# The 64-row remainder of the last product: two tiles of tokens in the two halves of TensorE's rows, in a kernel of attention, MLP and a block-quantised gated FFN

## The chip, the cores and the metric

The kernel runs on one core of a Trainium2 chip. The time is that of the device in microseconds (us) for one execution. The profiler gives the span from the first to the last instruction of one execution, in the same unit.

## What is computed

Eight sequences of 512 tokens with 256 features go through one layer, everything in float32. Per sequence: a layernorm; causal self-attention in which queries, keys and values are all the normed input; a residual layernorm; cross-attention to 64 context rows; another; an MLP of 256 to 1024 to 256 with relu; another; the sum with the input. Then comes the gated FFN, in which this case lies:

```
zq   = fp4(layernorm(x))                       # blocks of 16: scale, rounding to 8 levels, back
h    = silu(zq @ fp4(w_gate).T) * (zq @ fp4(w_up).T)      # 256 -> 704
out  = x + fp4(h) @ fp4(w_down).T                         # 704 -> 256
```

The inner width is 704 = 5 x 128 + 64. TensorE sums over its 128 rows, so the last product (704 to 256) is five full blocks of rows and a rest of 64.

## The kernel before, in words

**Tiling.** A sequence is a batch of four tiles of 128 tokens (NT = 4); there are B = 8 batches, hence 32 tiles. In the code I = 704, P = 128, D = 256, WI = I // P = 5 full blocks, RI = 64 the rest, NI = 6 blocks with the padded one.

**The last product (L1087 to L1112, `last`).** For each tile `product` issues NI = 6 matmuls into one bank of PSUM: the stationary operand is a block of hqT (704 inner features by 128 tokens, the turned and quantised h), the moving one a block of wd (inner features by 256 outputs). Block 6 holds 64 real rows and 64 rows of zeros in both. VectorE then adds the bank to x (L1102), and SyncE (SP) issues the store of the tile to the output (L1109). A float32 matmul stands in the profile as two MATMUL records, each after a LDWEIGHTS record of its own: 32 tiles x 6 x 2 = 384 records.

**How hqT is turned.** In batches 0 to 6 (`down`, L1038), ScalarE splits h into planes of 16 bits (L1047), SP stores the 704 columns of both planes to a DRAM buffer hd (L1053), and a transposing DMA reads hd back as hqT (L1058). There are three buffers hd; their last 64 columns are set to zero once at the start (`pads`, L1122, from a tile `nothing`, L384). In batch 7 TensorE turns h by products with an identity (L416 and L1078), and ScalarE evicts them (L1071, L1081, L1082); the zero rows of hqT come from three memsets at the start (L377). The weights w_down go the same way through hd into wd (L710, L715).

**What sets the order.** The kernel is written as operations with an engine, a cost and the buffers that they read and write. `Plan.order` (L190) simulates the engines with these costs and picks, on each engine, the operation with the lowest key whose inputs are there and whose buffers are free. The key comes from due times (`DUE`, L43, one for each batch and stage; stage 4 is the last product), drawn back through the chain of successors (`_keys`, L151), plus a push (L1139: the weights of the FFN; `LOAD_EARLY`, L42: the loads of x and context). Each kind of buffer has a number of homes, and some have quotas (L310 to L346). So costs, due times and numbers of homes fix the order in which the instructions of each engine stand; at run time each engine works through its list, waiting on semaphores. PSUM has eight banks of one kind, "bank", shared by all products.

The costs in the plan: `pe(cols)` (L56) is 0.429 us for a matmul of 256 moving columns; a tile's last product is 6 x 0.429 us. A turned block costs 0.112 us (L419).

One other product in this kernel doesn't fill TensorE's rows: `columns` (L721) turns the bias b1, an array of 8 rows by 128, once at the start (L730).

Of the kernel before, what the change touches and what calls it, by code (L numbers as in the profile page):

```python
# [12 lines left out]
U16 = mybir.dt.uint16  # L13
AF = mybir.ActivationFunctionType
ALU = mybir.AluOpType
# [4 lines left out]
P = 128  # L20
# [18 lines left out]
TURN = 2.6  # L39

BY_PRODUCTS = (4, 2, 1)
LOAD_EARLY = 2150.0  # L42
DUE = [  # L43
    [-1573.0, 346.0, 1086.0, -75.0, 155.0],
    [-342.0, 966.0, 145.0, -67.0, 387.0],
    [69.0, 825.0, -138.0, 835.0, 418.0],
    [2022.0, 515.0, -83.0, 958.0, 279.0],
    [963.0, 1398.0, 889.0, 514.0, -531.0],
    [101.0, -947.0, -373.0, -1174.0, -419.0],
    [-595.0, -1611.0, -583.0, -368.0, -313.0],  # L50
    [-1468.0, -811.0, -1127.0, -1471.0, -2197.0],
    [-2350.0],
]


def pe(cols):  # L56
    return 2 * max(0.109, cols * PE_PASS)
# [201 lines left out]
def kernel(  # L259
# [52 lines left out]
    z_homes = several("z", 8, [P, D + 2])  # L312
    plan.kind("y0", y0_homes)
    plan.kind("z", z_homes)
    plan.kind("zT", several("zT", 6, [P, ND, SZ]))
    plan.kind("turned", several("turned", 3, [P, ND, S]), ordered=False)
    plan.share("y0T", "turned", 3)
# [4 lines left out]
    plan.kind("xp", several("xp", 12, [P, NT, SZ]))  # L322
    xpT_homes = several("xpT", 1, [P, S])
    plan.kind("xpT", xpT_homes)
    plan.kind("hT", several("hT", 10, [P, S]))
    plan.kind("zq", several("zq", 1, [P, NT, D]))
    plan.kind("zm", several("zm", 2, [P, NT * D]), ordered=False)
    plan.kind("wide", several("h", 7, [P, NI * P]), ordered=False)
    plan.share("h", "wide", 5)
    plan.share("hm", "wide", 2)  # L330
    plan.share("wq", "wide", 5)
    hqT_homes = several("hqT", 3, [P, NI * P])
# [8 lines left out]
    plan.kind("ln", several("ln", 11, [P, 48]), ordered=False)  # L341
# [25 lines left out]
    ident = fixed("ident", [P, P])  # L367
# [5 lines left out]
        nc.gpsimd.memset(t[:SZ, D:], 1.0)  # L373
    for t in xpT_homes:
        nc.gpsimd.memset(t[SZ:, :], 0.0)

    for t in hqT_homes:  # L377
        nc.gpsimd.memset(t[RI:, WI * P :], 0.0)
    squares = fixed("squares", [P, D])
    mhalf = fixed("mhalf", [P, NT])  # L380
    nc.vector.memset(mhalf, -0.5)


    nothing = fixed("nothing", [P, 2, NI * P - I], U16)  # L384
    nc.gpsimd.memset(nothing, 0)


# [12 lines left out]
    wd = fixed("wd", [P, NI, D])  # L400

    plan.kind("const", ["const"] * 13, ordered=False)
    ready = {}
# [214 lines left out]
    def planes_of(v, n):  # L618
        return v.bitcast(U16).rearrange("p (g h k) -> p g h k", k=n, h=2)

    def weights():
# [4 lines left out]
        for j, w in enumerate((w_gate, w_up)):  # L626
            for half, groups in enumerate(((0, 1), (2, 3, 4))):
                v = plan.buf("wq")
                wide = len(groups) * D
# [17 lines left out]
                m = fp4(v, lambda v=v, n=n: v.ap[:, :n], "wq", n // BLOCK)  # L647
                g = len(groups)
                d = plan.buf("zd")

                def apart(v=v, m=m, n=n, wide=wide):
# [11 lines left out]
                    reads=[m], writes=[d], lag=1.1,  # L663
# [7 lines left out]
                    reads=[d], writes=[(ready["wgu"], (j, half))], lag=TURN,  # L671
                )
                if not half:
                    d = plan.buf("rest")
# [5 lines left out]
                        reads=[m], writes=[d], lag=1.5,  # L680
# [12 lines left out]
        for r in range(ND):  # L693
            v = plan.buf("wq")
            plan.op(
                "SP", 1.8, lambda v=v, r=r: nc.sync.dma_start(v.ap[:, :I], w_down[ts(r, P), :]),
                writes=[v],
            )
            m = fp4(v, lambda v=v: v.ap[:, :I], "wq", NBI)
            d = plan.buf("hd")  # L700
            plan.op(
                "ACT", act(2 * I),
                lambda v=v, m=m: nc.scalar.copy(
                    planes_of(m.ap[:, :I], I), halves(v.ap[:, :I], I)
                ),
                reads=[v], writes=[m],
            )
# [287 lines left out]
    def glu(b, xs, s):  # L995
# [5 lines left out]
        zT = plan.buf("zqT")  # L1001
# [36 lines left out]
        def down(t, h):  # L1038
            plan.stage = 4
            m = fp4(h, lambda h=h: h.ap[:, :I], "hm", NBI)  # L1040
            hqT = plan.buf("hqT")
            if b < B - 1:
                hd = plan.buf("hd")
                planes = lambda: m.ap[:, :I].bitcast(U16).rearrange("p (h k) -> p h k", h=2)
                plan.op(
                    "ACT", act(2 * I),
                    lambda: nc.scalar.copy(  # L1047
                        planes(), h.ap[:, :I].bitcast(U16).rearrange("p (k h) -> p h k", h=2)
                    ),
                    reads=[h], writes=[m],  # L1050
                )
# [12 lines left out]
            else:  # L1064
                turned_by_products(h, hqT)
            last(t, hqT)

        def turned_by_products(h, hqT):
# [16 lines left out]
            plan.op("ACT", 0.36, evict, reads=[pt], writes=[(hqT, 1)])  # L1085

        def last(t, hqT):  # L1087
            op = plan.buf("bank")

            def product(hqT=hqT, op=op):  # L1090
                for c in range(NI):
                    nc.tensor.matmul(  # L1092
                        op.ap[:, :D], hqT.ap[:, ts(c, P)], wd[:, c, :],
                        start=(c == 0), stop=(c == NI - 1),
                    )

            plan.op(
                "PE", NI * pe(D), product, reads=[(hqT, 0), (hqT, 1), ready["wd"]], writes=[op]
            )
            plan.op(  # L1100
                "DVE", 0.42,
                lambda t=t, op=op: nc.vector.tensor_tensor(  # L1102
                    xs.ap[:, t, :], op.ap[:, :D], xs.ap[:, t, :], ALU.add
                ),
                reads=[op], writes=[(xs, t)],
            )
            plan.op(
                "SP", 0.7,
                lambda t=t: nc.sync.dma_start(out[b, ts(t, P), :], xs.ap[:, t, :]),  # L1109
                reads=[(xs, t)],  # L1110
            )


        if b == B - 1:
# [7 lines left out]
    def pads():  # L1122

        for t in hd_homes:
            nc.sync.dma_start(t[:, :, I:], nothing)


    columns()
# [4 lines left out]
        writes=[ready["w1"]],  # L1133
# [47 lines left out]
```

## Time and profile before

| what | value |
|---|---|
| time, median of 3 runs | 584.24 us (583.91 to 584.69) |
| the profiled execution: its own time | 584.01 us |
| the profiled execution: its span | 582.0 us |
| TensorE busy | 570.7 us, 98% of the span |
| VectorE, ScalarE, GpSimd busy | 77%, 62%, 11% |
| the last product (L1092): records | 384 matmuls, 86.7 us busy |
| one of them: record / start to start | 380 ns / 215.8 ns |
| share of the 16 DMA engines | 45.6% |

PE in the profile is TensorE's matmuls, PEld its weight loads, DVE VectorE, ACT ScalarE, POOL GpSimd, SPq the queue of SyncE, which issues all the DMAs here. A form such as 128\*64 gives the rows and columns of TensorE's array that an instruction uses. Matmuls are pipelined: a record of 380 ns overlaps the next, so the price of one in a stream is the distance between two starts. The chain of waits gives it: twelve records of L1092 take 2.59 us there, 215.8 ns each. The profile calls "chain" the work that ended last, followed back from the last instruction; an engine that is in the chain for 96% of the span sets the time nearly alone.

### The profile page before, as it was taken

What the parts mean: (1) busy time and instruction counts of PE and PEld (TensorE: products, weight loads), DVE (VectorE), ACT (ScalarE), POOL (GpSimd) and SP (SyncE); (2) the same over time, 40 slices, a digit from 0 to 9 for tenths busy, and PEclk for the clock granted to TensorE, in tenths of its full rate; (3) what the DMA queues carried; (4) which work ended last, traced back from release to release, by engine and by line L of the source; (5) the groups of instructions that cost most, each with busy time, mean ns of one, the idle gap of its engine ahead of it and who ended that gap; (6) DMA issues with size and microseconds to landing.
All of it is one profiled execution on the core that took longest, in us unless ns stands there. A gap on an engine that the chain in (4) does not pass through costs nothing.

```text
span 582.0 us, 7151 instructions
## 1 busy us (share of the span) xinstructions
PE 570.7 (98%) x2273; PEld 409.2 (70%) x2273; DVE 447.5 (77%) x1125; ACT 359.6 (62%) x751; POOL 61.4 (11%) x102
## 2 busy tenths in 40 slices
PE   4999999999999999999999999999999999999997
PEld 2787485876697647678667777848578756877686
DVE  4799976979837998354998978978473897589892
ACT  4667948589748675444577777765953766345431
POOL 5222101022001000000201010000110100000000
PEclk9999999999999999999999999999999999999999
DMA  7930394462660257303338665655328042435421
GB/s 161 242 101 2 95 210 116 118 158 46 173 149 19 72 125 201 98 9 82 98 106 180 187 141 133 134 151 141 97 62 179 11 110 67 114 89 142 124 51 64
DMA packets 142581, 66.37 MB, mean 114 GB/s; under 512 B 107848, under 2 KB 142032, under 8 KB 142544
## 3 DMA queue, kind: packets, MB, share of 16 engines
q1 hardware_dynamic: 142544, 65.92, 45.6%
q8 instruction: 18, 0.29, 0.2%
q14 instruction: 19, 0.16, 0.1%
HBM read 9.90 MB, written 29.66 MB: 68 GB/s over the span
## 4 chain that ended last, share of the span: by engine, by line
PE 96%; DVE 1%; DMA 1%; ACT 1%; SPq 0%; POOL 0%; issue 0%; DVEq 0%
PE bank L1012 26%; PE bank L957 19%; PE bank L937 19%; PE bank L1092 14%; PE bank L797 6%; PE bank L764 5%; PE bank L915 2%; PE bank L876 2%; PE bank L416 2%; DMA z<-in_ctx_dram 1%; ACT squares L485 0%; SPq L356 0%; DVE x L554 0%; ACT turned L828 0%; DVE r L534 0%; POOL ln L500 0%
## 5 line engine op out<-in xcount | busy, mean ns | idle before, releaser
L1012 PE MATMUL bank<-wgu,turned 128*128 128x352 f32 x512 | 155.5, 459 | 0.0
L1012 PEld LDWEIGHTS bank<-wgu,turned 128*128 128x128 f32 x512 | 96.6, 190 | 50.4 <-issue 0.5
L957 PE MATMUL bank<-w,hT 128*128 128x256 f32 x512 | 112.6, 379 | 0.0
L937 PE MATMUL bank<-turned,w 128*128 128x512 f32 x256 | 111.5, 592 | 0.0
L957 PEld LDWEIGHTS bank<-w,hT 128*128 128x128 f32 x512 | 97.0, 190 | 14.5 <-issue 1.2
L937 PEld LDWEIGHTS bank<-turned,w 128*128 128x128 f32 x256 | 48.6, 190 | 57.4 <-issue 52.6
L1092 PE MATMUL bank<-wd,hqT 128*128 128x256 f32 x384 | 86.7, 380 | 0.0
L1092 PEld LDWEIGHTS bank<-wd,hqT 128*128 128x128 f32 x384 | 72.6, 190 | 12.5 <-issue 1.0
L600 DVE SCALAR_TENSOR_TENSOR h<-h,h 128x704 f32<-128x704 f32 (+2 forms) x76 | 66.7, 882 | 12.0 <-ACT h L594 11.7
L485 ACT ACTIVATE squares<-r,ln 128x256 f32<-128x256 f32 x96 | 48.8, 508 | 40.4 <-DVE ln L477 38.2
L500 POOL TENSOR_TENSOR ln<-ln,mhalf 128x4 f32<-128x4 f32 x32 | 36.5, 1139 | 351.7 <-DVE ln L493 351.7
L945 ACT ACTIVATE hT<-bank,cols 128x512 f32<-128x512 f32 x64 | 42.6, 682 | 17.0 <-PE bank L937 16.5
L1024 ACT ACTIVATE h<-bank 128x352 f32<-128x352 f32 x64 | 28.4, 457 | 34.8 <-PE bank L1012 34.4
L1047 ACT COPY h<-h 128x1408 uint16<-128x1408 uint16 x28 | 38.0, 1362 | 17.6 <-DVE h L607 17.5
L594 ACT ACTIVATE h<-h 128x704 f32<-128x704 f32 (+2 forms) x38 | 30.0, 789 | 26.6 <-DVE h L588 23.7
L968 DVE SCALAR_TENSOR_TENSOR r<-bank,r 128x256 f32<-128x256 f32 x32 | 13.4, 420 | 41.9 <-PE bank L957 41.9
L764 PE MATMUL bank<-turned 128*128 128x512 f32 (+3 forms) x128 | 38.1, 444 | 0.3 <-ACT turned L828 0.3
L797 PE MATMUL bank<-y,e 128*128 128x258 f32 x160 | 36.9, 382 | 0.1
L1031 DVE TENSOR_TENSOR h<-h,bank 128x352 f32<-128x352 f32 x64 | 32.1, 512 | 5.7 <-PE bank L1012 2.9
L607 DVE TENSOR_TENSOR h<-h,q 128x704 f32<-128x704 f32 (+2 forms) x38 | 33.5, 884 | 0.4
L588 DVE SCALAR_TENSOR_TENSOR h<-h,q 128x704 f32<-128x704 f32 (+2 forms) x38 | 33.5, 882 | 0.4
L797 PEld LDWEIGHTS bank<-y,e 128*128 128x128 f32 x160 | 29.9, 190 | 5.4 <-POOL e L784 0.5
(89 smaller groups left out, 664.5 us busy)
## 6 DMA issues: line engine op xcount, KB each, us to landing
zd<-zm SPq DMA_DIRECT2D x25, 512.0 KB, 2.9
hd<-h SPq DMA_DIRECT2D x30, 352.0 KB, 2.7
out_dram<-x SPq DMA_DIRECT2D x32, 128.0 KB, 1.7
x<-in_x_dram SPq DMA_DIRECT2D x7, 512.0 KB, 4.6
w<-in_L_xattn_w_dram SPq DMA_DIRECT2D x2, 1024.0 KB, 11.3
zd<-h SPq DMA_DIRECT2D x2, 384.0 KB, 2.8
h<-in_L_ffn_w_down_dram SPq DMA_DIRECT2D x2, 352.0 KB, 3.1
x<-in_x_dram SPq DMA_DIRECT2D x4, 128.0 KB, 2.2
```

The source lines that it names most:

```text
L485: lambda t=t: nc.scalar.activation(squares, view(t), AF.Square, bias=s.ap[:, 24 + t : 25 + t], accum_out=s.ap[:, 28 + t : 29 + t],),
L500: lambda: nc.gpsimd.tensor_tensor(s.ap[:, 36:40], s.ap[:, 32:36], mhalf, ALU.pow),
L588: lambda: nc.vector.scalar_tensor_tensor(blocks_of(view()), blocks_of(view()), TIE, each(rc()), ALU.mult, ALU.mult),
L600: lambda reverse=reverse, f=f: nc.vector.scalar_tensor_tensor(view(), mm(), LEAST, view(), ALU.max, f, reverse1=reverse),
L764: nc.tensor.matmul(sc.ap[:, :n], yT.ap[:, c, ts(k, P)], yT.ap[:, c, k * P :], start=(c == 0), stop=(c == ND - 1),)
L797: nc.tensor.matmul(av.ap[:, : D + 2], e.ap[:, ds(start[k] + (t - k) * P, P)], y0.ap[:, k, :], start=(k == 0), stop=(k == t),)
L937: nc.tensor.matmul(hp.ap, w1_sb[:, c, ts(f, P)], yT.ap[:, c, :], start=(c == 0), stop=(c == ND - 1),)
L945: lambda f=f, hp=hp, h=h: nc.scalar.activation(h.ap, hp.ap, AF.Relu, bias=b1_sb[:, f : f + 1]),
L957: nc.tensor.matmul(fp.ap[:, :D], hT[f].ap[:, ts(t, P)], w2_sb[:, f, :], start=(f == 0), stop=(f == NF - 1),)
L1012: nc.tensor.matmul(gp.ap[:, :HI], zT.ap[:, c, ts(t, P)], wgu[:, c, ds(j * I + n * HI, HI)], start=(c == 0), stop=(c == ND - 1),)
L1047: lambda: nc.scalar.copy(planes(), h.ap[:, :I].bitcast(U16).rearrange("p (k h) -> p h k", h=2)),
L1092: nc.tensor.matmul(op.ap[:, :D], hqT.ap[:, ts(c, P)], wd[:, c, :], start=(c == 0), stop=(c == NI - 1),)
```

## The change

1. **The product.** The five full blocks of a tile remain one operation of TensorE. The rest of 64 rows is no longer padded. When both tiles of a pair (0 and 1, 2 and 3) have their five blocks, a new operation `rests` issues for each a matmul over 64 rows only: the even tile's in rows 0 to 63 of the array, the odd tile's in rows 64 to 127, each into its own bank. The plan's cost of `rests` is 0.63 us. Only after it come the two additions on VectorE and the two stores of the output.
2. **Where the rest lies.** For odd tiles it must lie in rows 64 to 127 of hqT. The store into hd is then two DMAs instead of one (five blocks, and the rest 64 columns further on); for batch 7 the odd tile's second turned block takes 128 columns that end with the rest, and the eviction takes the upper half. In wd the rest lies in both halves: one more DMA for each of the two stores of w_down.
3. **The start.** The three memsets of hqT go; the zeros in hd are 128 columns wide instead of 64.
4. **The plan.** New due times, pushes, and numbers of homes: zT 6 to 7, xp 12 to 10, hT 10 to 9, wide 7 to 8, hm 2 to 3, wq 5 to 4, hqT 3 to 4, ln 11 to 13, y0T's quota 3 to 1.

```diff
-LOAD_EARLY = 2150.0
+LOAD_EARLY = 2634.0
 DUE = [
...
-    for t in hqT_homes:
-        nc.gpsimd.memset(t[RI:, WI * P :], 0.0)
...
-    nothing = fixed("nothing", [P, 2, NI * P - I], U16)
+    nothing = fixed("nothing", [P, 2, P], U16)
...
-                lambda m=m, d=d: nc.sync.dma_start(d.ap[:, :, :I], planes_of(m.ap[:, :I], I)[:, 0]),
+                lambda m=m, d=d: [
+                    nc.sync.dma_start(d.ap[:, :, :I], planes_of(m.ap[:, :I], I)[:, 0]),
+                    nc.sync.dma_start(
+                        d.ap[:, :, I:], planes_of(m.ap[:, :I], I)[:, 0, :, WI * P :]
+                    ),
+                ],
...
+                def store():
+                    if t % 2:
+                        nc.sync.dma_start(hd.ap[:, :, : WI * P], planes()[:, :, : WI * P])
+                        nc.sync.dma_start(hd.ap[:, :, I:], planes()[:, :, WI * P :])
+                    else:
+                        nc.sync.dma_start(hd.ap[:, :, :I], planes())
+
                 plan.op(
-                    "SP", 1.4, lambda: nc.sync.dma_start(hd.ap[:, :, :I], planes()),
+                    "SP", 1.4 + 0.5 * (t % 2), store,
...
             def rest(h=h, pt=pt):
-                for c in range(4, NI):
-                    cw = min(P, I - c * P)
-                    nc.tensor.transpose(pt.ap[:cw, ts(c - 4, P)], h.ap[:, ds(c * P, cw)], ident)
+                nc.tensor.transpose(pt.ap[:, :P], h.ap[:, ts(4, P)], ident)
+                lo = I - RI * (1 + t % 2)
+                nc.tensor.transpose(pt.ap[: I - lo, ts(1, P)], h.ap[:, lo:I], ident)
...
-                nc.scalar.copy(hqT.ap[:RI, ds(WI * P, P)], pt.ap[:RI, ts(WI - 4, P)])
+                half = ts(t % 2, RI)
+                nc.scalar.copy(hqT.ap[half, ds(WI * P, P)], pt.ap[half, ts(1, P)])
...
             def product(hqT=hqT, op=op):
-                for c in range(NI):
+                for c in range(WI):
                     nc.tensor.matmul(
                         op.ap[:, :D], hqT.ap[:, ts(c, P)], wd[:, c, :],
-                        start=(c == 0), stop=(c == NI - 1),
+                        start=(c == 0), stop=False,
                     )
...
+            pair.append((t, hqT, op))
+            if len(pair) < 2:
+                return
+            two = list(pair)
+            pair.clear()
+            def rests():
+                for t, hqT, op in two:
+                    half = ts(t % 2, RI)
+                    nc.tensor.matmul(
+                        op.ap[:, :D], hqT.ap[half, ds(WI * P, P)], wd[half, WI, :],
+                        start=False, stop=True,
+                    )
+            plan.op(
+                "PE", 0.63, rests, reads=[(q, 1) for _, q, _ in two],
+                writes=[o for _, _, o in two],
+            )
+            for t, hqT, op in two:
...
-            nc.sync.dma_start(t[:, :, I:], nothing)
+            nc.sync.dma_start(t[:, :, WI * P :], nothing)
...
-    plan.push = 5681.0
+    plan.push = 8884.0
```

More of the change, by code (lines that the diff above doesn't have):

```diff
@@ L41 @@
 BY_PRODUCTS = (4, 2, 1)
-LOAD_EARLY = 2150.0
+LOAD_EARLY = 2634.0
 DUE = [
[L44 to L52, printed above, removed]
+    [-1972.0, 451.0, 1026.0, -71.0, 390.0],
+    [-366.0, 1145.0, 287.0, -63.0, 448.0],
+    [-84.0, 957.0, -115.0, 759.0, 489.0],
+    [2198.0, 240.0, -81.0, 1231.0, 322.0],
+    [2074.0, 1527.0, 1434.0, 1260.0, -3.0],
+    [531.0, -18.0, 233.0, -763.0, 298.0],
+    [132.0, -1150.0, -257.0, 407.0, 387.0],
+    [261.0, 24.0, -783.0, -585.0, -670.0],
+    [-2984.0],
 ]
@@ L314 @@
     plan.kind("z", z_homes)
-    plan.kind("zT", several("zT", 6, [P, ND, SZ]))
+    plan.kind("zT", several("zT", 7, [P, ND, SZ]))
     plan.kind("turned", several("turned", 3, [P, ND, S]), ordered=False)
-    plan.share("y0T", "turned", 3)
+    plan.share("y0T", "turned", 1)
     plan.share("yT", "turned", 3, ordered=False)
@@ L321 @@
     plan.kind("r", several("r", 3, [P, NT, D]))
-    plan.kind("xp", several("xp", 12, [P, NT, SZ]))
+    plan.kind("xp", several("xp", 10, [P, NT, SZ]))
     xpT_homes = several("xpT", 1, [P, S])
     plan.kind("xpT", xpT_homes)
-    plan.kind("hT", several("hT", 10, [P, S]))
+    plan.kind("hT", several("hT", 9, [P, S]))
     plan.kind("zq", several("zq", 1, [P, NT, D]))
     plan.kind("zm", several("zm", 2, [P, NT * D]), ordered=False)
-    plan.kind("wide", several("h", 7, [P, NI * P]), ordered=False)
+    plan.kind("wide", several("h", 8, [P, NI * P]), ordered=False)
     plan.share("h", "wide", 5)
-    plan.share("hm", "wide", 2)
-    plan.share("wq", "wide", 5)
-    hqT_homes = several("hqT", 3, [P, NI * P])
+    plan.share("hm", "wide", 3)
+    plan.share("wq", "wide", 4)
+    hqT_homes = several("hqT", 4, [P, NI * P])
     plan.kind("hqT", hqT_homes)
@@ L340 @@
     plan.kind("zd", zd_homes, ordered=False)
-    plan.kind("ln", several("ln", 11, [P, 48]), ordered=False)
+    plan.kind("ln", several("ln", 13, [P, 48]), ordered=False)
     plan.kind("q", several("q", 6, [P, 3, 64]), ordered=False)
@@ L1064, in down, with turned_by_products @@
             else:
-                turned_by_products(h, hqT)
+                turned_by_products(t, h, hqT)
             last(t, hqT)
-        def turned_by_products(h, hqT):
+        def turned_by_products(t, h, hqT):
             transposed(
@@ L1075, in rest @@
             def rest(h=h, pt=pt):
-                for c in range(4, NI):
-                    cw = min(P, I - c * P)
-                    nc.tensor.transpose(pt.ap[:cw, ts(c - 4, P)], h.ap[:, ds(c * P, cw)], ident)
+                nc.tensor.transpose(pt.ap[:, :P], h.ap[:, ts(4, P)], ident)
+                lo = I - RI * (1 + t % 2)
+                nc.tensor.transpose(pt.ap[: I - lo, ts(1, P)], h.ap[:, lo:I], ident)
             def evict(pt=pt, hqT=hqT):
                 nc.scalar.copy(hqT.ap[:, 4 * P : WI * P], pt.ap[:, : (WI - 4) * P])
-                nc.scalar.copy(hqT.ap[:RI, ds(WI * P, P)], pt.ap[:RI, ts(WI - 4, P)])
+                half = ts(t % 2, RI)
+                nc.scalar.copy(hqT.ap[half, ds(WI * P, P)], pt.ap[half, ts(1, P)])
             plan.op("PE", 0.27, rest, reads=[h], writes=[pt], takes=[hqT])
             plan.op("ACT", 0.36, evict, reads=[pt], writes=[(hqT, 1)])
+        pair = []
         def last(t, hqT):
@@ L1090, in product @@
             def product(hqT=hqT, op=op):
-                for c in range(NI):
+                for c in range(WI):
                     nc.tensor.matmul(
                         op.ap[:, :D], hqT.ap[:, ts(c, P)], wd[:, c, :],
-                        start=(c == 0), stop=(c == NI - 1),
+                        start=(c == 0), stop=False,
                     )
             plan.op(
-                "PE", NI * pe(D), product, reads=[(hqT, 0), (hqT, 1), ready["wd"]], writes=[op]
-            )
-            plan.op(
[L1101 to L1105, printed above, removed]
-            )
[L1107 to L1111, printed above, removed]
+                "PE", WI * pe(D), product, reads=[(hqT, 0), (hqT, 1), ready["wd"]],
+                writes=[op],
+            )
+            pair.append((t, hqT, op))
[10 more added lines that the diff above has]
+                    )
+            plan.op(
+                "PE", 0.63, rests, reads=[(q, 1) for _, q, _ in two],
+                writes=[o for _, _, o in two],
+            )
+            for t, hqT, op in two:
+                plan.op(
+                    "DVE", 0.42,
+                    lambda t=t, op=op: nc.vector.tensor_tensor(
+                        xs.ap[:, t, :], op.ap[:, :D], xs.ap[:, t, :], ALU.add
+                    ),
+                    reads=[op], writes=[(xs, t)],
+                )
+                plan.op(
+                    "SP", 0.7,
+                    lambda t=t: nc.sync.dma_start(out[b, ts(t, P), :], xs.ap[:, t, :]),
+                    reads=[(xs, t)],
+                )
         if b == B - 1:
```

## The prediction

> **What bounds the kernel now.** I read the engines' shares first, then the chain that ended last, then who made TensorE wait, then the only place where TensorE works on fewer than 128 rows.
>
> ```profile
> PE 570.7 (98%) x2273; PEld 409.2 (70%) x2273; DVE 447.5 (77%) x1125; ACT 359.6 (62%) x751; POOL 61.4 (11%) x102
> ...
> PEclk9999999999999999999999999999999999999999
> ...
> PE 96%; DVE 1%; DMA 1%; ACT 1%; SPq 0%; POOL 0%; issue 0%; DVEq 0%
> ...
> L1092 PE MATMUL bank<-wd,hqT 128*128 128x256 f32 x384 | 86.7, 380 | 0.0
> ```
>
> TensorE is busy 98% of the span, makes up 96% of the chain, and runs at its full clock in all slices. The last product, L1092, never waits: 0.0 us idle before 384 records.
>
> ```profile
> PE bank L416 <- DMA z<-in_ctx_dram: 7.7, 2, 6.2
> ...
> PE bank L764 <- ACT turned L828: 0.3, 1, 0.3
> ```
>
> These two lines of the view of waits are all that TensorE waits for: 7.7 us for the context at the start, and 0.3 us once. In the chain TensorE runs from 10.8 to 578.8 us without a break, so the time moves one for one with the work on TensorE, and what the other engines do counts only where it makes TensorE wait, or at the two ends.
>
> **The work on TensorE.** In the chain twelve records of L1092 take 2.59 us, 215.8 ns from start to start. The padded sixth matmul is two of them, and a pair of tiles has four: 4 x 215.8 = 863 ns. There are 32 tiles, 16 pairs. The change takes these 13.8 us away and puts 16 operations `rests` in their place, each four records again of the same 256 columns, but over 64 rows. The whole question is how long one takes, and that has two unknowns.
>
> *Do the two halves run side by side?* No two neighbouring matmuls of this trace use different halves of the rows, so bound it: two slots of 215.8 ns if each record of one tile lies beside one of the other (432 ns), four if none does (863 ns). The order of issue decides between them. Each matmul is two records one behind the other, so the list is A first, A second, B first, B second. Matmul starts follow the program's order in this trace. Then A second must wait for A first, which holds the same rows; B first can start beside A second; B second must wait for B first. That is three slots, 647 ns, also the middle of the bounds. I take it.
>
> *What does the change of rows cost?* One instruction of this trace works on fewer than 128 rows, the turning of the bias (L730, 8 rows). These are lines of the timeline around it:
>
> ```profile
> 15.82 0.50 PE L764 MATMUL bank<-turned 128*128 128x128 f32 x3
> 15.93 0.19 PEld L764 LDWEIGHTS bank<-turned 128*128 128x128 f32 x1
> ...
> 16.24 0.14 PEld L730 LDWEIGHTS bank<-ident,c_rows 8*128 8x128 f32 x1
> 16.25 0.23 PE L730 MATMUL bank<-ident,c_rows 8*128 8x8 f32 x1
> 16.41 0.19 PEld L797 LDWEIGHTS bank<-y,e 128*128 128x128 f32 x1
> 16.41 0.70 PE L797 MATMUL bank<-y,e 128*128 128x258 f32 x2
> ```
>
> Columns: start, time, engine, line. Elsewhere the weights of the next matmul load as the present one starts: the load at 15.93 belongs to the last matmul of L764, which starts at 16.04 (end 16.32 less its 275 ns). The load for L730 doesn't start then, but 204 ns later, and L730's matmul with it; nor does the load for L797 run ahead, it starts at 16.41 with its own matmul. The next matmul of L797 starts only at 16.73 (end 17.11 less 0.38), 321 ns on where 217 is usual. From the start at 16.04 to that at 16.73 are 691 ns. Without L730 they would be 109 (usual for this form) + 217 = 326. So the excursion costs 365 ns, of which its own stream of 8 columns is 8/256 of 215.8, 7 ns. The other **358 ns** are two switches: the array runs empty (97 ns more than usual going in, about 53 coming out) and the weights load in the open (321 - 217 = 104 ns, twice). Neither load waited for data: the bias had landed at 10.4 us, and the part of `e` that L797's first matmul reads was done at 14.7.
>
> It is one place, and 8 rows, not 64; so bound it from both sides. The lower end is nothing: the 36 turned blocks of form 128\*64 (L416 and L1078) alternate with 128\*128 at the usual 109 ns, loads ahead, so a change of columns costs nothing. The upper end is 358 ns for each `rests`. I take 358, since L730 is the only row in which the number of *rows* changes, and it does so both ways.
>
> So a `rests` is 647 + 358 = 1005 ns where 863 stood: 142 ns more, x 16 = **+2.3 us**.
>
> Two rules of the Trainium skill bear on this. "TensorEngine Tiling (Array Packing)", section Tiling Modes, says that a change of the tiling mode drains TensorE, while a mere change of tile doesn't; it speaks against this change. L730 agrees (358 ns), the 128\*64 blocks don't. "TensorE: Matmul & The Clock Gate", Part 3, has matmuls on different rows start some 4 ns apart, with a span of about one matmul for the pack; no run here shows it. Taken for the whole pair, and without the drain, that would be 432 + 4 ns and -6.8 us. The sum above needs neither.
>
> **The other parts.**
> - *Order.* All due times and the numbers of homes change, so every engine's list does. From 10.8 us on the old order leaves TensorE 0.3 us idle, so a new one can gain no more than that there. It could lose: the even tile's bank is held until the odd tile's product is done (the chain has products of neighbouring tiles 9.5 to 16 us apart), so seven of eight banks turn over. A bank of L937 is filled in 859 ns and emptied by ScalarE in 682 ns (L945), so three suffice. I take 0, ends -0.3 and +1.0.
> - *The split store.* 14 odd tiles get one more DMA on SP, of the kind that takes 566 ns to issue (L1053, median), 7.9 us in all; behind it in SP's list stand the transposing read of the same tile, the other tiles' and outputs' DMAs. What hides it: hqT lands 4.0 us after its issue, and TensorE waits for none of the 28. The tightest, issued at 554.3, lands about 558.3, for a product at 560.6: 2.3 us of slack against 0.6. If all that cover were gone, 14 x 0.57 = 7.9 us would be the price; I take 0. The two further stores for w_down, pads of twice the width and the copies of batch 7 (same number, same widths) go with it, at 0.
> - *The waits of `rests`.* It needs both products, which stand ahead of it on TensorE and have already waited for both hqT. So nothing new can hold up what is queued behind it.
> - *The start.* Three memsets go from GpSimd, 0.5 us just ahead of its first power (L455 at 6.54), on which the first normed tiles hang (ScalarE, 7.50); the wider zeros give back some 0.2. TensorE waits for the fourth normed tile at 9.2 for 0.32 us. I take -0.2. With the new order of loads it may be -1.1 (TensorE's first y at 8.05, where the first tile is normed, instead of 8.77, and those 0.3) to +1.0 (two more DMAs ahead of the context, 0.4 to 0.6 us each).
> - *The end.* Before, the last addition (0.42 us) starts at 578.85 and the span ends at 582.0. Now tiles 2 and 3 finish together and VectorE adds them one behind the other. The first bank is ready one or two slots before the second, so the last addition moves by 0 to 0.42 us. I take +0.2.
>
> Sum against the profiled execution's 584.01 us: 2.3 + 0 - 0.2 + 0.2 = +2.3, **586.3 us**. The median before, 584.24, is 0.2 us above that execution, so the same number stands for the median. About 0.2% (1.2 us) is what a measurement of this kernel can tell from no change.
>
> **The rivals.**
> - *A. Switches cost as at L730, three slots*: the forecast, 585.4 to 587.4. **0.47.** (If the array empties in 53 ns both ways, 1.6 us instead of 2.3.)
> - *B. The switch to 64 rows is free, three slots*: 647 - 863 = -216 ns x 16 = -3.5 us, **580.5**. It is the case on the other side, and one mechanism: whether the first load over 64 rows, and the first over 128 after it, run ahead. It decides from 216 ns: a round trip cheaper than that makes the change a gain. For it: the free change of columns, and the plan's cost of 0.63 us for `rests`, near 647, where `pe(256)` = 0.429 is near the measured 0.432. Against it: L730. **0.28.**
> - *C. Switches cost, and the halves don't run side by side*: 863 + 358 - 863 = +358 x 16 = +5.7, 589.7. For it: no two matmuls of this trace run in one slot. **0.09.**
> - *D. Switches cost, and the halves overlap fully*: 432 + 358 = 790, -73 x 16 = -1.2, 582.8. Against it: the order of issue. **0.07.**
> - *E. The change doesn't do what it says*: no overlap, no price of switches: 584.0. **0.05.**
> - *F. Full overlap, free switches*: -6.9, 577.1. **0.04.**
>
> **The numbers.** Forecast A: 586.3. The range leaves out C, F and the ends of the rest: from B with 0.6 us of the start's lower end, 579.9, to A with the upper ends of the banks (+1.0) and the start (+1.2 over what I took), 588.5. Cases of both signs hold most of it: A alone is 585.4 to 587.4. Slower by over 0.2%: A but its lower edge, and C, 0.54. Within 0.2%: E, half of D, the edge of A, 0.10. Faster: B, F, half of D, 0.36.
>
> **What would show it.** In the timeline of the changed kernel, around a group of records over 64 rows: whether its first load starts with the last 128-row matmul (B) or some 0.3 us later (A); whether the third record starts a few ns after the second (three slots) or 216 ns (C); the distance from the first 64-row start to the next 128-row one. L1092's follower should have 320 records, and the 64-row line 64. TensorE must still have no wait in the middle of the span. The prediction is wrong if the loads run ahead, if the order of the four records isn't as I take it, or if TensorE starts to wait for banks.

## The result, and the profile after

| | before | after |
|---|---|---|
| time, median of 4 runs each on one chip | 584.47 us (583.91 to 584.74) | 588.25 us (587.62 to 588.27) |
| ratio, 95% interval | | 1.0063 (1.0046 to 1.0081) |
| the profiled execution: its time / its span | 584.01 / 582.0 us | 588.26 / 586.5 us |

The change makes the kernel slower by 3.8 us, more than a measurement can mistake. The forecast was 586.3, slower, with a range to 588.5, so direction and range held. The way to it didn't: two of its steps were wrong by 3 and 5 us, in opposite directions.

These are lines of the page after, those that answer to the ones shown of before. The last product is now L1105 (five blocks) and L1124 (the pair, `rests`).

```profile
PE 571.1 (97%) x2273; PEld 400.8 (68%) x2273; DVE 447.3 (76%) x1125; ACT 363.0 (62%) x753; POOL 61.3 (10%) x99
...
PEclk9999999999999999999999999999999999999999
...
PE 86%; DVE 4%; DMA 4%; ACT 3%; POOL 1%; SPq 1%; issue 1%; DVEq 0%; POOLq 0%; ACTq 0%
...
L1105 PE MATMUL bank<-wd,hqT 128*128 128x256 f32 x320 | 73.8, 381 | 0.0
```

TensorE's busy time is 0.4 us more, the span 4.5 us. TensorE makes up 86% of the chain where it made up 96%: DMA, VectorE and ScalarE have come into it. So the first place to look is not the new operation but who makes TensorE wait (columns: us in total, times, longest):

```profile
PE bank L412 <- DMA z<-in_ctx_dram: 7.2, 2, 5.1
PE bank L798 <- POOL e L785: 1.4, 1, 1.4
PE bank L1013 <- DMA turned<-zd: 1.3, 1, 1.3
PE bank L765 <- DMA turned<-zd: 0.8, 1, 0.8
PE bank L916 <- ACT xpT L901: 0.4, 1, 0.4
PE bank L938 <- DVE h L596: 0.4, 1, 0.4
PE bank L877 <- DMA turned<-zd: 0.2, 1, 0.2
```

The first line is the start, as before. Below it before had one wait of 0.3 us; now there are six, at 26.3 (POOL), 49.0 (xpT), 127.7, 340.1, 374.2 and 449.4 us, together 4.5 us. None is at `rests`.

Now the new operation itself, in the timeline around one pair (start, time, engine, line, records), first the matmuls, then the weight loads:

```profile
270.38 0.81 PE L1105 MATMUL bank<-wd,hqT 128*128 128x256 f32 x3
271.13 0.70 PE L1124 MATMUL bank<-wd,hqT 64*128 64x256 f32 x4
271.76 0.86 PE L1013 MATMUL bank<-wgu,turned 128*128 128x352 f32 x2
```

```profile
270.60 0.19 PEld L1105 LDWEIGHTS bank<-wd,hqT 128*128 128x128 f32 x1
271.12 0.30 PEld L1124 LDWEIGHTS bank<-wd,hqT 64*128 64x128 f32 x4 [0.33 <-issue]
271.76 0.59 PEld L1013 LDWEIGHTS bank<-wgu,turned 128*128 128x128 f32 x3 [0.33 <-issue]
```

The loads show the two switches, as the prediction's last part described them: the loads over 64 rows don't run ahead, they start with their own matmuls at 271.12, 0.33 us after the load before has ended; the next load over 128 rows waits 0.33 us again, until 271.76. Within the group the four matmul records start at 271.126, 271.132, 271.446 and 271.452 us: two together, and 314 ns later two together. That is two slots, not three.

To price the pair, I measure from the last start over 128 rows ahead of it to the first regular step behind it. The last L1105 starts at 270.816, and the second L1013 at 272.156 (271.76 + 0.86, less its 461 ns): 1340 ns, of which 216 for that L1105 and 296 for the first L1013 are usual. **828 ns** are the pair's. It splits so: 310 ns from the last L1105 to the first L1124, 94 more than usual, in which the array runs empty; 320 from the first to the third record, one slot of 216 and 104 of a weight load in the open; 310 from the third to the load of L1013, one slot and 94 of running empty again; and 400 from the first L1013 to the second, 104 more than usual, another open load. 94 + 320 + 310 + 104 = 828. Thirteen of the 15 pairs in the stream cost 828 to 831 ns; two, which are followed by turned blocks, 755. The padded form costs 863. The end of the last pair, where no switch back follows, is left out.

**Where the 4.5 us of span come from**, all against the profile before. The start is 0.34 us earlier (the first matmul of 512 columns at 10.44 us instead of 10.78). From there to the end of TensorE's last record are 4.4 us more; in them the pairs give back 0.9 us (13 x 33 ns, twice 108 ns, and 0.23 us for the last pair, behind which no switch back follows), so waits and gaps take 5.3 us more (the view of waits books 4.2 of it as waits). The end is 0.5 us longer (3.64 us from the end of TensorE's last record to the end of the span, 3.16 before). The sum, -0.3 - 0.9 + 5.3 + 0.5, is the span's growth to 0.1 us.

### The profile page after: what moved, and what is told of

The parts are those of the page before. It is cut to its first block, busy times and chain, and to the rows that moved or that the text cites. A ratio compares the mean times of both kernels' runs of the same rounds, so it can differ in the third digit from the quotient of the medians.

```text
span 586.5 us, 7179 instructions
## 1 busy us (share of the span) xinstructions
PE 571.1 (97%) x2273; PEld 400.8 (68%) x2273; DVE 447.3 (76%) x1125; ACT 363.0 (62%) x753; POOL 61.3 (10%) x99
## 4 chain that ended last, share of the span: by engine, by line
PE 86%; DVE 4%; DMA 4%; ACT 3%; POOL 1%; SPq 1%; issue 1%; DVEq 0%; POOLq 0%; ACTq 0%
PE bank L1013 23%; PE bank L958 19%; PE bank L938 19%; PE bank L1105 11%; PE bank L798 5%; PE bank L765 3%; DMA turned<-zd 2%; PE bank L916 2%; ACT squares L481 2%; PE bank L1124 2%; DMA v_beta<-in_L_xattn_beta_dram 1%; PE bank L877 1%; PE bank L412 1%; DVE r L909 1%; SPq L741 0%
## 5 line engine op out<-in xcount | busy, mean ns | idle before, releaser
L1013 PE MATMUL bank<-wgu,turned 128*128 128x352 f32 x512 | 156.7, 461 | 1.3 <-DMA turned<-zd 1.3
L1013 PEld LDWEIGHTS bank<-wgu,turned 128*128 128x128 f32 x512 | 96.1, 190 | 54.9 <-issue 3.4
L1105 PE MATMUL bank<-wd,hqT 128*128 128x256 f32 x320 | 73.8, 381 | 0.0
L1105 PEld LDWEIGHTS bank<-wd,hqT 128*128 128x128 f32 x320 | 60.1, 190 | 12.5 <-issue 2.5
L1025 ACT ACTIVATE h<-bank 128x352 f32<-128x352 f32 x64 | 28.4, 456 | 26.6 <-PE bank L1013 26.3
L765 PE MATMUL bank<-turned 128*128 128x512 f32 (+3 forms) x128 | 38.3, 447 | 0.8 <-DMA turned<-zd 0.8
```

The costliest lines, as they stand in the source:

```text
L765: nc.tensor.matmul(sc.ap[:, :n], yT.ap[:, c, ts(k, P)], yT.ap[:, c, k * P :], start=(c == 0), stop=(c == ND - 1),)
L1013: nc.tensor.matmul(gp.ap[:, :HI], zT.ap[:, c, ts(t, P)], wgu[:, c, ds(j * I + n * HI, HI)], start=(c == 0), stop=(c == ND - 1),)
L1105: nc.tensor.matmul(op.ap[:, :D], hqT.ap[:, ts(c, P)], wd[:, c, :], start=(c == 0), stop=False,)
```

## The experiments

My theory after the result: (1) a pair costs 830 ns because the halves overlap and two switches cost some 395; (2) the slowdown is the new order of the work, which makes TensorE wait, and not the pair. The rivals: the pairs' switches cause the waits; or three slots plus a cheaper switch make up 830; or the new stores on SP make the late transfers. All ratios are against the kernel before in runs on the same chip; the runs stand on several chips, so a difference between the medians of two of them is rougher than their ratios.

### What a pair costs: e1, e2

e1 keeps every list of the kernel after and takes `rests` over all 128 rows; e2 keeps 64 rows, but both tiles in the lower half.

```diff
-                        op.ap[:, :D], hqT.ap[half, ds(WI * P, P)], wd[half, WI, :],
+                        op.ap[:, :D], hqT.ap[:, ds(WI * P, P)], wd[:, WI, :],      # e1
-                    half = ts(t % 2, RI)
+                    half = ts(0, RI)                                               # e2
```

> The changed kernel with every engine's list of instructions as it is, but the operation `rests` multiplies over all 128 rows (its sums take in 64 stale rows, so its output is not the reference's). My theory now: the two halves run fully side by side, and a pair costs about 830 ns with its two switches of rows, against 863 ns over full rows; the rest of the slowdown comes from the order, where TensorE waits in the middle of the span for 5 to 6 us. So here: the switches are gone, a pair takes 863 ns, the waits stay: 588.5 to 589.2 us, 0.3 to 0.9 over the changed kernel. Rival, the three slots of the prediction (1005 ns a pair): 142 x 16 = 2.3 us less, 586.0. Rival, the waits come from the switches: they go, about 584.

> The changed kernel with the same lists, but both matmuls of `rests` use rows 0 to 63 (the odd tile's sum takes stale rows, so the output is not the reference's). If the halves really run side by side in the changed kernel, here they can't: four slots, 863 + about 395 of switches = 1260 ns a pair, 430 more, 6.9 us over 16, of which the waits in the middle can take up some: 591 to 595 us. If four records take two slots for another reason than the halves, a pair stays at 830 ns and the time at 588.3.

e1: 588.87 us, 1.008 (1.0065 to 1.0095). e2: 593.05 us, 1.0149 (1.0134 to 1.0164). The chain of waits through the same pair, first of e1, then of e2, then of the kernel after (start, us, line, records):

```profile
269.32 2.16 PE bank L1105 x10
271.48 0.86 PE bank L1123 x4
272.35 2.37 PE bank L1013 x8
```

```profile
269.09 2.16 PE bank L1105 x10
271.25 1.06 PE bank L1124 x4
272.31 2.56 PE bank L1013 x8
```

```profile
269.04 2.16 PE bank L1105 x10
271.19 0.63 PE bank L1124 x4
271.83 2.56 PE bank L1013 x8
```

The full rows take 0.86 us, and their loads run ahead: no switch. With both tiles in one half the starts are 320, 216 and 216 ns apart, four slots, and the entry grows by 0.43 us, exactly two slots. So it is the second half of the rows that saves two slots, not one; "three slots" is refuted, and so is a cheaper switch. The medians of e1 and of the kernel after are 0.6 us apart, but the intervals of their ratios overlap, so the worth of the pairs rests on the traces: 0.9 us for all 16, of which the end (3.20 us in e1, 3.64 in the kernel after) takes back 0.4.

The chain also shows a trap. Its entry of 0.63 us runs from the first record over 64 rows to the next load; the 93 ns of running empty stand with L1105, the open load with L1013 (2.56 us for eight records, where e1 has 2.37). The plan's 0.63 equals this number, and it is 0.2 us short of the price.

In e1 the waits are still there (POOL 1.6, turned 1.4, 0.7 and 0.5, xpT 0.4 us), all but the one of 0.4 us for `h`: they don't come from the switches. In e2, where TensorE needs 6.9 us more for its pairs, the time grows by only 4.8 us, and the waits at 340, 374 and 449 us shrink to 0.3 us or less; the one at 127.7, ahead of all pairs, stays (1.1 us). What TensorE waits for runs beside it at its own pace.

### How far the overlap goes: e7, e8

Each pair's two products are issued twice, in turn (A, B, A, B; e7) or grouped (A, A, B, B; e8).

```diff
-                for t, hqT, op in two:
+                for n, k in enumerate((0, 1, 0, 1)):      # e8: (0, 0, 1, 1)
+                    t, hqT, op = two[k]
```

> The changed kernel with the same lists, but `rests` issues its two matmuls twice, in the order A, B, A, B (the rest is counted twice in the output). If the two halves work through their own matmuls side by side: four slots, 864 + about 395 for the switches = 1260 ns, so a second pair within one change of rows costs 432 ns instead of 830. The time: 16 x 0.43 = 6.9 us more, less what the waits take up.

> As the run before, in the order A, A, B, B. The question is how far a matmul of one half passes those of the other that stand ahead of it. If it passes any: four slots, 1260 ns. If only the one record right ahead of it: six slots or nearly, 1475 to 1690 ns.

One execution each, so without an interval: 592.63 and 593.30 us. In the traces two pairs in one switch cost 1262 ns (e7) and 1268 (e8): one switch, four slots, both times. In e7 the starts are 6, 315, 6, 209, 7, 209 and 7 ns apart. In e8 the first record of B starts about 13 ns after the first of A, ahead of three records of A that stand before it in the program. (The records don't name their half; that two within 13 ns are one of each follows from e2, where records of one half stand 216 ns apart.) That is the point at which the forecast's order of issue failed: a matmul isn't held up by earlier ones on the other half. And the price of a switch is per excursion: a second pair in the same one costs 432 ns.

### Which part of the order: e3, e4, e9

The waits for `turned` (the turned zq) looked like a buffer that came free too late: the chain goes from TensorE's L765, which reads `turned`, to the DMA.

```profile
119.01 4.36 PE bank L798 x20
123.37 1.70 PE bank L765 x4
125.06 4.22 DMA turned<-zd
129.28 0.14 issue
129.42 1.42 PE bank L1013 x4
```

So e3 gives `turned` a fourth piece of memory, over which the three homes rotate. e4 takes the additional store of the odd tiles away (a rival: more DMAs on SP).

```diff
+                if k["of"] == "turned":                     # e3
+                    self.spare.append(b.home)
+                    b.home = self.spare.pop(0)
...
-                    if t % 2:                               # e4
+                    if False:
```

> The changed kernel with the same lists, but the buffers `turned` go round over four pieces of memory instead of three (the plan still counts three). Theory: three of the waits in the middle (at 127.7, 340 and 449 us, 2.8 us together) are transposing DMAs that start only when TensorE has read the last of the three buffers, and then take 4.2 to 4.5 us; with a fourth they start earlier: 585.5 us (584.8 to 586.5), the other waits stay. Rival, the queue of SP or the transfers themselves are late: 588.3, the waits stay.

> The changed kernel, but odd tiles store h in one DMA, as even ones do (their rest lands in rows 0 to 63, the product takes stale rows, so the output is not the reference's). Theory: the 14 extra DMAs cost TensorE nothing: within 0.5 us of 588.3. Rival, the split stores hold up SP's queue and so the transposing DMAs: 1 to 4 us less.

e3: 587.61 us, 1.0065 (1.0042 to 1.0089), the same waits (1.4, 0.9 and 0.3 us). My theory of the buffer fell. SP's own timeline in the kernel after shows what the chain's inferred releaser hides:

```profile
121.31 0.57 SPq L847 DMA_DIRECT2D zd<-zm  x1
125.06 1.78 SPq L852 DMA_TRANSPOSE turned<-zd  x1
```

The transposing read at 125.06 waits for the store of the same data, issued at 121.31. From there to the landing at 129.28 are 8.0 us, where the plan counts 1.9 + 1.1 + 1.8 + 2.6 = 7.4.

That store is itself late. Ahead of it in SP's list stands the transposing read of w_down (L716), and this waits 1.9 us for the second of the two stores (L708) that the change put in place of one. Two lines of the timeline, and L708 in the view of DMAs (KB, us to landing):

```profile
114.93 0.61 SPq L708 DMA_DIRECT2D hd<-h  x1
119.75 1.50 SPq L716 DMA_TRANSPOSE wd<-hd  x1
```

```profile
hd<-h SPq DMA_DIRECT2D x1, 32.0 KB, 4.3
```

The median of the 16 stores of this size is 2.3 us. In e7, whose lists are the same up to there, L708 lands after 2.4 us, L716 starts at 117.42, and the wait at 127.7 is gone. The DMA packets of the traces tell these runs apart: in the kernel after, e1, e2, e3, e4 and e8, all with that wait, a packet of 16 KB of the instruction queue starts between 116.8 and 117.3 us, and the last 16 packets of L708 start behind it (at 118.2 in the kernel after); in e7 and e9 it comes at 113.8 and 114.2, ahead of L708. That the one delays the other is not shown by a run of its own.

e4: 593.25 us, 1.0147 (1.0124 to 1.017). TensorE's waits at 26, 127.7, 340 and 449 us are all there (1.5, 1.1, 1.2 and 2.5 us), so the second stores of the odd tiles aren't their cause; the second stores of w_down stay in e4, and it says nothing of them. The time is longer for another reason. These are windows of the trace (us; busy time of PE, PEld, DVE, ACT and POOL; then the granted clock, the share of the DMA engines and GB/s):

```profile
449.00:452.00 3.00, 0.88 (x3) 0.21 (x2) 1.77 (x5) 2.53 (x6) 1.17 (x1) 1.00 1.09 155
452.00:456.00 4.00, 3.61 (x17) 3.64 (x18) 0.00 (x0) 0.00 (x0) 0.00 (x0) 0.54 0.00 0
456.00:459.00 3.00, 3.00 (x7) 1.75 (x7) 2.21 (x10) 2.44 (x6) 0.00 (x0) 0.50 0.00 0
459.00:462.00 3.00, 3.00 (x14) 2.08 (x13) 0.52 (x1) 0.52 (x2) 0.00 (x0) 0.97 0.00 0
```

TensorE waited 2.5 us for one `turned`, whose store took 4.9 us from issue to the read, and then worked 7 us at about half its clock. All four executions of e4 have a mean clock of 0.994 to 0.997; one of e3's ten has 0.994 too (593.45 us), the others 0.999 or 1. Why that store landed so late I can't say from the trace.

e9 shortens the chain itself: from the second use of a buffer on, the store of zq takes two of the four tiles.

```diff
+            lo = NT // 2 if id(d.ap) in seen else 0
...
+                d.ap[lo:].rearrange("t p h k -> p t h k"), planes()[:, lo:]
```

> The changed kernel with the same lists, but from the second use of each DRAM buffer zd on, the store ahead of a transposing DMA writes only two of the four tiles (the other two keep old values, so the output is not the reference's). Theory: the waits of TensorE at 127.7, 340 and 449 us are the end of the chain store and transposing read, which takes about 8 us, runs beside TensorE's list and is 0.4 to 1.5 us too long for it; half the store is some 0.5 us shorter, so each of these waits shrinks by about that, 1.0 to 1.5 us in all: 586.8 to 587.3. Rival, TensorE waits there for the reader of a buffer or for SP's queue: the waits stay, 588.3.

585.69 us, 1.002 (1.001 to 1.003): 1.5 us over before in place of 3.8, so 2.3 us are gone. The page's DMA issues (KB each, us from issue to landing), and the waits of TensorE:

```profile
zd<-zm SPq DMA_DIRECT2D x21, 256.0 KB, 2.2
```

```profile
PE bank L412 <- DMA z<-in_ctx_dram: 5.3, 1, 5.3
PE bank L412 <- POOL ln L451: 1.7, 1, 1.7
PE bank L798 <- POOL e L785: 1.6, 1, 1.6
PE bank L925 <- ACT xpT L910: 0.4, 1, 0.4
```

The halved stores land after 2.2 us instead of 3.2, and in the profiled execution (584.8 us, 0.9 faster than the median) all waits for DMAs in the middle are gone. Not all of this is the halving. The store ahead of 127.7 us is a first use of its buffer and full here too (512 KB, 3.5 us to landing); it goes out at 119.60, 1.7 us earlier, because L708 landed after 2.5 us, as in e7. That makes 1.4 of the 3.5 us by which this span is shorter than that of the kernel after. The other 2.1 come at 340 us and later, behind halved stores. I had expected a gain of 1.0 to 1.5 us, as I had taken the store to be shortened by half of that. So the waits for `turned` at 340 and 449 us come from a chain of store and transposing read that this order starts too late, and the one at 127.7 from the late L708 at the head of such a chain. The waits for POOL and xpT stay, as they should; they weren't tried by themselves.

### Other orders: e5, e6

e5 is the kernel before, padded, with nothing but other due times, which the plan holds for nearly as good (580.1 us against 579.7). e6 is the change with 0.83 us as the plan's cost of `rests` and due times found anew for it (plan 579.8).

```diff
-                "PE", 0.63, rests, reads=[(q, 1) for _, q, _ in two],
+                "PE", 0.83, rests, reads=[(q, 1) for _, q, _ in two],       # e6
```

> The kernel before, padded product and all numbers of homes as they are; only its due times are moved about, to an order that the plan holds to be nearly as good (580.1 us in the plan, 579.7 for the kernel before). Theory: most of the slowdown of the changed kernel is the new order, in which chains that the plan prices too low come late for TensorE; then another order of the unchanged kernel must lose microseconds too: 586 to 591 us, with 2 to 6 us of TensorE's waits in the middle of the span where the kernel before has 0.9. Rival, orders that the plan holds equal are equal on the chip: 584.6, and the waits of the changed kernel belong to the change.

> The changed kernel with 0.83 us as the plan's cost of `rests` instead of 0.63, and due times, pushes found anew for that cost (579.8 us in the plan, the plan of the kernel before 579.7). Theory: the price of `rests` in the plan has little to do with TensorE's waits; this order is again another, so 584 to 590 us, and its distance to the kernel before is its waits in the middle of the span less 0.6 us. Rival, the waits come from the false 0.63 us: with the honest price they go, 583.6.

e5: 585.91 us, 1.0022 (1.0012 to 1.0032), with waits of 1.8 us for `turned` in two places. It lies below what I expected (586 to 591), but shows the direction: new due times alone, without any change of the work, cost 1.3 us. e6: 585.39 us, 1.0015 (1.0005 to 1.0025): with another order the same pairs lose 0.8 us instead of 3.8. Price and order changed together here, so the run doesn't tell which of them helped. Waits remain in its profiled execution: 1.4 us for DMAs, 1.1 us for ScalarE and 0.7 for VectorE, and after the wait of 1.1 us the clock fell to 0.54 for 3 us. That execution (586.85 us, mean clock 0.997) is one of two such among the ten; the other eight have a clock of 1.0 and 584.43 to 585.65 us.

### A version that beats both? e10, e11, e12

If a switch is paid per excursion, four tiles in one are cheaper than two pairs: 1262 ns against 2 x 863 = 1726 padded, 0.46 us for each batch. To hold no four banks until then, `product` closes its sum after five blocks, VectorE adds it as before, and the four rests go into two banks of their own, with two more additions. hqT gets six homes.

```diff
+            if len(four) < NT:
+                return
+            rb = [plan.buf("bank") for _ in range(2)]
...
+                        rb[t % 2].ap[:, ts(t // 2, D)], hqT.ap[half, ds(WI * P, P)],
+                        wd[half, WI, :], start=True, stop=True,
...
+                "PE", 1.26, rests, reads=[(q, 1) for _, q in four], writes=rb,
```

e10 does so in all batches (plan 579.8); e11 and e12 keep pairs in the last batch, and take two sets of due times that hold up in the plan when transfers take 0.3 or 0.6 us longer (plan 577.3 and 577.5).

> A try at more than the change: the rests of all four tiles of a batch in one operation, within one change of rows, into two banks of their own that VectorE adds to x (two more additions per batch, hqT in six buffers), with due times found anew (579.8 us in the plan, as for the kernel before). TensorE's price by the runs so far: 1262 ns for four tiles where the padded product has 1726: 3.7 us less over eight batches. Against it stand the order's own waits and an end that is some 2 us longer, since two more additions and four stores come after the last product. Theory: 583 to 588 us. If the saving on TensorE were all that counts: 580.8.

> As the run of four tiles in one operation, but the last batch works in pairs (a shorter end), and the due times were chosen for an order that stays good when the transfers take 0.3 and 0.6 us longer than the plan's cost (577.3 us in the plan against 579.7 for the kernel before). Theory: if the lost time of the changed kernel is TensorE waiting for chains that the plan prices too low, an order with slack in them keeps most of the 3.4 us that TensorE is spared (464 ns x 7 batches, and some 70 ns for the last): 581.5 to 583.5 us, with under 2 us of waits in the middle of the span. Rival, the waits belong to the operation over halves and its held buffers: 585 us or more, as the first try.

> The same kernel with a second set of due times, found apart from the first in the same way (577.5 us in the plan). It tells how far one order's luck goes: theory 581.5 to 584.5 us; rival 585 us or more.

e10: 585.29 us, 1.0022 (1.0012 to 1.0032); the four tiles do cost 1262 ns, but in the profiled execution, the slowest of ten (586.65 us), TensorE waits 3.4 us for `turned`, and the end takes 5.0 us after its last record, where the kernel before has 3.2. e11: **583.28 us, 0.9987 (0.9978 to 0.9996)**, 11 runs. e12: 583.72 us, 0.9992 (0.998 to 1.0003), not told from before. The waits of e11:

```profile
PE bank L412 <- DMA z<-in_ctx_dram: 7.1, 1, 7.1
PE bank L1013 <- DMA turned<-zd: 1.2, 1, 1.2
PE bank L938 <- DMA turned<-zd: 1.1, 1, 1.1
```

e11 is ahead of both kernels, of the one before by 0.13% as the ratio has it (the medians are 1.2 us apart), with an interval that ends just short of no change. Seven batches give 3.2 us on TensorE (7 x 0.46), and 2.3 us of waits take most of it back. From e10 to e11 2.0 us went; slack in the plan and the other end of the last batch came together there, so the share of each isn't shown, and the waits weren't removed.

## Why the prediction was right and wrong

- **"Three slots, 647 ns": wrong.** "B first can start beside A second" followed from starts in the order of the program. B first starts 6 ns after A first, ahead of A second (the kernel after, e7 and e8, with e1 and e2 as controls). Two slots, 216 ns a pair less than forecast.
- **"358 ns, two switches": right in kind, 10% low.** With two slots, 828 - 432 = 396 ns. The open loads are the 104 ns taken from L730, twice; running empty is 94 ns in (97 taken) and 94 out (53 taken). One excursion of 8 rows foretold those of 64.
- **The pair** is thus rival D, to which I gave 0.07: -0.9 us measured, -1.2 forecast. Rival B (the switch is free) fell at the loads. The plan's 0.63, which I counted for B, equals a distance that leaves out the costs booked to the neighbours.
- **"Order: I take 0, ends -0.3 and +1.0": wrong, and the largest error.** It measured about +5.3 us. I weighed banks, and no wait is for banks or at `rests`. What I didn't price are chains beside TensorE that have no slack in the new order, such as a store and a transposing read of 8.0 us that start when SP's list lets them. e1 keeps the lists and with them the waits; e6 has the same pairs with 3 us less in another order; e5 loses 1.3 us with a new order alone; e9 gives some 2 us back by shortening the chain.
- **The split store at 0: right for the odd tiles, wrong for w_down.** Without the odd tiles' second stores (e4) the waits stay. But the "two further stores for w_down", which I let go with them at 0, hold one that landed after 4.3 us, and the wait of 1.3 us at 127.7 hangs on it; it is part of the 5.3.
- **The waits of `rests` at 0: right.** In the page L1105 and L1124 have no wait for data.
- **Start -0.2 and end +0.2:** -0.34, within what was said, and +0.5, just above the upper end of 0.42: the two banks are ready within 7 ns of each other, not one or two slots apart.

Sum by the steps: -0.9 instead of +2.3, +5.3 instead of 0, -0.3, +0.5. The two large errors, -3.2 and +5.3, left some 2 us between 586.3 and 588.25. The number was near by luck, the direction too: with D's price and my "order 0" I would have said about 583 and faster. By the signs that it named itself the prediction failed: the order of the four records isn't as I took it, and TensorE waits in the middle of the span.

On the rules of the Trainium skill that the prediction weighed: "TensorEngine Tiling (Array Packing)", Tiling Modes, has a change of mode drain TensorE; for a change of rows the runs agree: TensorE runs empty for 94 ns each way, and with the open loads both ways take 396 ns. "TensorE: Matmul & The Clock Gate", Part 3, has matmuls on different rows start some 4 ns apart with a span of about one matmul. Here the starts are 6 to 7 ns apart, a little more, and each two records share one slot of 216 ns (e7), which agrees.

**Open:** why this order makes TensorE wait for GpSimd's `e` (1.4 to 1.6 us in after, e1, e3, e4 and e9) and for xpT; no run took these away alone. What delays L708, and how the kernel after would do without it: a packet of instructions ahead of its last ones is seen, but not tried. Why one store in e4 took so long. How much of the 0.8 and 1.5 us that e6 and e9 still take over the kernel before would go with another order again.

## What to carry to other kernels

Price an operation from the last regular start ahead of it to the first regular one behind it: its own records and its entry in the chain (0.63 us) leave out what it does to its neighbours (0.83). Changing TensorE's rows cost 396 ns per excursion here, so put as much as possible into one: a pair saves 0.03 us on the padded form, four tiles 0.46. Where an engine is busy 98% of the time and the order comes from a plan, a change brings a new order with it, and that can cost more than the change saves; to price the change hold the order (e1 against after), and to price the order look for chains whose landing is counted to the tenth of a microsecond, and follow each wait back to the first late transfer on the queue, not only to the last.

## What the runs showed of the hardware

- Matmuls on different halves of the rows pass each other against the program's order, also past three earlier ones (e8: 13 ns between the first starts; four slots either way).
- A change of rows and back costs 396 ns (94 + 104 + 94 + 104), a change of columns (the turned blocks, which keep their step of 109 ns) nothing.
- The granted clock can fall after short waits: to 0.5 for 7 us behind a wait of 2.5 us (e4), and to 0.54 for 3 us behind one of 1.1 us (e6). Waits of 1.4 us in the kernel after left it at 1.00.
- A store of half the bytes (256 instead of 512 KB) landed 1.0 us earlier, 2.2 us after its issue instead of 3.2.
- The same store of 32 KB (L708) landed after 2.4 and 2.5 us where a 16 KB packet of the instruction queue came ahead of it (e7, e9), and after 4.3 us where this packet came among its own (the kernel after, e1).
